# Ordering the second attention of a gated cross-attention block by whole heads

## The chip, the cores and the metric

The kernel runs on one core of a Trainium2 chip. The metric is the device time of one execution in microseconds (us). The engines are named as the profile names them: PE (TensorE, matmuls; PEld is its weight load), DVE (VectorE), ACT (ScalarE), POOL (GpSimd) and SP (SyncE, which issues all DMAs here).

## The reference

Two blocks follow one another on x of 4 x 256 tokens x 256: each is a gated cross-attention and a gated feed-forward. The change lies in the cross-attention of the second block alone:

```python
B, T_text, T_vis = 4, 256, 1601          # N_HEADS 16, N_KV_HEADS 8, HEAD_DIM 128, D_TEXT 256, D_VISION 128
x = layernorm(x) before this call
q = (text_hidden @ Wq).reshape(B, T_text, N_HEADS, HEAD_DIM).transpose(0, 2, 1, 3)
k = (vision_tokens @ Wk).reshape(B, T_vis, N_KV_HEADS, HEAD_DIM).transpose(0, 2, 1, 3)
v = (vision_tokens @ Wv).reshape(B, T_vis, N_KV_HEADS, HEAD_DIM).transpose(0, 2, 1, 3)
k, v = repeat each twice along the heads
scores = einsum('bhtd,bhsd->bhts', q, k) / sqrt(HEAD_DIM)
scores = where(mask, scores, -inf)
out = einsum('bhts,bhsd->bhtd', softmax(scores), v)
return out.reshape(B, T_text, N_HEADS * HEAD_DIM) @ Wo     # x + tanh(g) * this
```

After it comes the second feed-forward, whose three weights are quantised to three values by their mean magnitude: `silu(x @ wu.T) * (x @ wg.T) @ wd.T`.

## The kernel before, in words

Four stages follow one another: the first attention, the first feed-forward, the second attention, and the second feed-forward, with loads and preparations laid between. The second attention runs from about 725 to 1604 us of the profiled execution. In it and in the stages around it, `keep_order` ties every engine's instructions to the order in which the program writes them, so the order of the Python calls is the order on each engine.

Before this stage the weights are folded head by head: `aq` is Wq times Wk transposed and divided by sqrt(128), `vo` is Wv times Wo. So a head needs a query of 128 context channels and attends to the 128 channels of the context itself. The unit of work is a head of one batch: `units` has 4 x 16 = 64 of them, numbered u.

The work of a head, by function and line (of the kernel before):

- `project(u)`, L1335: two matmuls on PE (each runs as two passes of 32-bit data) into `ps_m`; ACT copies the query to `qT` (L1336).
- `scores(u, t)`, L1346, for eight tiles t of 32 queries: the 1601 context rows are split in four sets of 401, and the four sets fill the four quarters of the 128 partitions. Four matmuls of 32 columns lie beside each other in PE's array and write one of four `ps_sc` buffers. DVE takes the tile out (L1353): it adds the mask, negates, writes `pr` and keeps the minimum in `nm`.
- `exponentials(u, t)`, L1361: ACT makes the exponentials in place and sums them into `nm`.
- `weigh_sets(u)`: the four sets of a query have each their own maximum and sum, which have to be brought to one. It has three steps. First, SP sends `nm` by four DMAs (L1370) to `bq`, so that a query's four sets lie side by side. Second, DVE finds the common extreme (`low`, L1373) and the differences (`ws`, L1375), and ACT makes their exponential (L1376). Third, DVE makes the weighted sum, its reciprocal and the factors (L1379 to L1382), and SP sends the factors `rs` back to 128 partitions by four DMAs (L1385). In the kernel before a fourth step follows: POOL multiplies `pr` by the factors, in two halves of four tiles (L1390).
- `turn(u, half)`, L1397: DVE transposes 32 x 32 blocks of half of `pr` into `pT`. There are three `pr` and two `pT`.
- `attend(u, k)`, L1404: 13 matmuls (26 passes) of the transposed context `cx` and `pT` into one half of the bank `ps_o`. `take(u)`, L1414: ACT copies the result to `ao`.
- `project_out(u)`, L1422: two matmuls with `vo` into `ps_y`, which gathers all heads of a batch; `add_out(b)`, L1433, adds it to x.

The order around these is written by hand. Time is cut in beats of half a head (four score tiles). In each beat PE gets four tiles, and then come the steps that `place` has put into the beat, in four places: MADE, THEN, TURNED and AFTER. With k = 2u the first beat of head u, DMAs of the sums come in beat k+1, the second step in k+2, the third and POOL's multiplication in k+3, the turns in k+4 and k+5, seven and six blocks of the output in k+6 and k+7, `take` in k+7, and `project_out` in k+8.

Work of other parts is spread over the beats in the same way: `layernorm_steps` and `token_parts` of a finished batch, `prepare_mask` (L1045 to L1059) and `prepare_ctx` (L1032 to L1039: POOL copies, PE transposes, ACT copies) for the next batch, and `quantise`, 26 steps that fetch the feed-forward's weights (`w_q`, L1279), sum their magnitudes on DVE (L1286), make the scales (L1289 to L1296) and the three-valued weights on DVE (L1304, L1305). In the kernel before a step of `quantise` stands at the end of every third half beat from beat 6 on.

Of the kernel before, what the change touches and what calls it, by code (L numbers as in the profile page):

```python
# [22 lines left out]
B, S, D = 4, 256, 256  # L23
# [9 lines left out]
H = 16  # L33
# [26 lines left out]
def tile_gated_cross_blocks(ctx: ExitStack, tc: tile.TileContext, a: dict, out: bass.AP):  # L60
# [202 lines left out]
    with ExitStack() as ph:  # L263
# [413 lines left out]
        made = {}  # L677
# [568 lines left out]
    with ExitStack() as ph:  # L1246
# [80 lines left out]
        queries, found, outs, ys = ({} for _ in range(4))  # L1327
# [37 lines left out]
        def weigh_sets(u):  # L1365
# [18 lines left out]
            for i in range(SETS):  # L1384
                nc.sync.dma_start(out=factors[i * TQ : (i + 1) * TQ], in_=w[:, i])  # L1385
            yield
            for half in range(2):
# [3 lines left out]
            yield  # L1391
# [44 lines left out]

        plan = {}
# [7 lines left out]
        MADE, THEN, TURNED, AFTER = range(4)  # L1445
        for u in range(2):
            project(u)
        for u, (b, h) in enumerate(units):
            k = 2 * u
            sets = weigh_sets(u)  # L1450
            place((k + 1, AFTER), once(sets))
            place((k + 2, AFTER), once(sets))
            place((k + 3, MADE), once(sets), once(sets))
            for half in range(2):
                place((k + 4 + half, TURNED), lambda u=u, half=half: turn(u, half))
            cut = (NB1 + 1) // 2
            for half, blocks in enumerate((range(cut), range(cut, NB1))):
                place((k + 6 + half, THEN), *(lambda u=u, n=n: attend(u, n) for n in blocks))
            place((k + 7, AFTER), lambda u=u: take(u))
            place((k + 8, AFTER), lambda u=u: project_out(u))  # L1460
            if u + 2 < len(units):
                place((k + 1, AFTER), lambda u=u: project(u + 2))
            if h == H - 1:
                place((k + 9, THEN), lambda b=b: add_out(b))
                norm = layernorm_steps(b, ps_m, "ps_m")
                for i in (0, 1, 2, 3):
                    place((k + 10 + i, AFTER), once(norm))
                parts = token_parts(b)
                for i in range(4):
                    place((k + 14 + i, AFTER), once(parts))  # L1470
            if h == H - 3 and b + 1 < B:
                ready = prepare_mask(b + 1)
                place((k, AFTER), once(ready))
                place((k + 2, AFTER), once(ready))
        for b in range(1, B):
            cx = prepare_ctx(b, ps_m, "ps_m")
            for i in range(8):
                place((2 * H * b - 4 + i, AFTER), once(cx))
# [131 lines left out]
```

## Time and profile before

| what | value |
|---|---|
| runs | 1671.71 us median of 3 (1671.45 to 1672.75) |
| the profiled execution | 1674.27 us |
| its span, first to last instruction | 1672.5 us |
| mean granted clock of PE | 0.979 |
| instructions | 34286 |
| DVE, POOL busy share of the span | 71%, 39% |
| second attention: first and last start of a score matmul (L1346) | 725.2 and 1571.4 us |
| end of L1382 of the fourth and of the last head | 778.53 and 1585.69 us |

The profiled execution has its own time, some 2.6 us above the median of the runs; durations are taken from it and differences are set against the median. A row of the timeline gives the start and the length in us, the engine (SPq is SP issuing DMAs), the line, the operation, the tiles as out<-in, the shape, how many instructions are merged, and in brackets how long the engine was idle before and what ended it. A row of the chain of waits gives start, length, engine, tile and line of the work that the end was waiting for. L numbers are lines of the kernel before.

### The profile page before, as it was taken

To read this page: it belongs to the slowest core of one execution; us is meant where nothing else is said; L and a number is where in the kernel's file an instruction comes from. 1 tells how busy PE (TensorE), PEld (TensorE's weight loads), DVE (VectorE), ACT (ScalarE), POOL (GpSimd) and SP (SyncE) were. 2 spreads that over 40 slices of the span, in tenths; PEclk is the share of its full clock that TensorE was granted. 3 is DMA by queue.
4 is the path that set the end of the run, shared out by engine and by line. 5 is a ranking of instruction groups with operands and counts; after the bars stand their busy time and mean duration, and the time that the engine had idled before them with its cause. 6 is when DMAs were issued, how large, how long until landed. Compare 5 with 4: busy or idle time off the path is not lost.

```text
span 1672.5 us, 34286 instructions
## 1 busy us (share of the span) xinstructions
PE 1561.6 (93%) x13273; PEld 910.2 (54%) x13282; DVE 1191.1 (71%) x2651; ACT 782.4 (47%) x1808; POOL 660.6 (39%) x755
## 2 busy tenths in 40 slices
PE   4389799999999999989999999999999999999998
PEld 1144454454455554445666666566665666666565
DVE  6687667766867636667777787777787777777645
ACT  1235545554565553444444444445444444444334
POOL 2524514612621215524444444445444454444420
PEclk9699999999999999999999999999999999999999
DMA  4422522430424132000000000000000000000000
GB/s 109 79 44 44 77 47 44 77 56 16 77 52 94 36 96 101 1 2 15 15 15 21 21 15 8 15 21 15 15 14 2 9 2 2 2 2 2 2 1 26
DMA packets 148467, 54.07 MB, mean 32 GB/s; under 512 B 133200, under 2 KB 143952, under 8 KB 148176
## 3 DMA queue, kind: packets, MB, share of 16 engines
q1 hardware_dynamic: 148304, 51.88, 14.9%
q8 instruction: 104, 1.70, 0.4%
q14 instruction: 59, 0.48, 0.1%
HBM read 24.30 MB, written 1.05 MB: 15 GB/s over the span
## 4 chain that ended last, share of the span: by engine, by line
PE 76%; DVE 12%; POOL 3%; ACT 3%; issue 3%; DMA 2%; SPq 1%; DVEq 0%; POOLq 0%; ACTq 0%
PE ps_o L1404 22%; PE ps_sc L1346 21%; PE ps_s L689 6%; PE ps_s L650 6%; PE ps_o L711 5%; PE ps_m L1335 3%; PE ps_y L1422 3%; DVE mxs L657 3%; PE ps_m L478 2%; PE ps_v L1169 2%; PE ps_a L1183 1%; POOL pr L1390 1%; PE ps_x L1114 1%; DVE hidden L1531 1%; DVE hidden L1528 1%
## 5 line engine op out<-in xcount | busy, mean ns | idle before, releaser
L1390 POOL TENSOR_TENSOR pr<-pr,rs 128x1604 f32<-128x1604 f32 x128 | 364.0, 2866 | 473.8 <-DMA rs<-ws 417.6
L1404 PE MATMUL ps_o<-pT,cx 128*128 128x256 f32 x1664 | 394.6, 388 | 4.3 <-DVE pT L1397 4.3
L1361 ACT ACTIVATE pr<-pr,nm 128x401 f32<-128x401 f32 x512 | 319.8, 626 | 131.3 <-DVE nm L1353 107.2
L1346 PE MATMUL ps_sc<-ctxT,qT 128*32 128x401 f32 x4096 | 374.6, 506 | 4.3 <-DVE nm L1353 4.3
L1404 PEld LDWEIGHTS ps_o<-pT,cx 128*128 128x128 f32 x1664 | 307.1, 190 | 123.0 <-issue 47.2
L1353 DVE CUSTOM_DVE_ANT_0 pr<-ps_sc,mk 128x401 f32<-128x401 f32 x512 | 286.6, 573 | 96.6 <-PE ps_sc L1346 71.7
L1397 DVE STREAM_TRANSPOSE pT<-pr 128x1664 f32<-128x1664 f32 x128 | 243.5, 1902 | 103.4 <-POOL pr L1390 103.4
L657 DVE TENSOR_REDUCE mxs<-ps_s 128x2 f32<-128x768 f32 (+1 forms) x256 | 246.2, 980 | 83.3 <-PE ps_s L650 82.6
L697 ACT ACTIVATE e<-ps_s 128x1024 f32<-128x1024 f32 (+1 forms) x224 | 214.7, 964 | 174.2 <-PE ps_s L689 173.3
L1346 PEld LDWEIGHTS ps_sc<-ctxT,qT 128*32 128x32 f32 x4096 | 120.8, 110 | 205.0 <-issue 145.8
L650 PE MATMUL ps_s<-kT,qTs 64*128 64x384 bf16 (+1 forms) x1536 | 176.3, 343 | 37.4 <-DMA qTs<-qp 14.9
L689 PE MATMUL ps_s<-qTs,kT 64*128 64x256 bf16 x2496 | 174.7, 271 | 10.6 <-DVE mxs L657 10.6
L689 PEld LDWEIGHTS <-kT 64*128 64x128 bf16 x2496 | 125.3, 95 | 56.5 <-issue 22.5
L650 PEld LDWEIGHTS <-qTs 64*128 64x128 bf16 x1536 | 66.3, 97 | 136.2 <-issue 92.9
L1376 ACT ACTIVATE ws<-ws 32x32 f32<-32x32 f32 x64 | 14.6, 228 | 211.9 <-DVE ws L1375 211.9
L711 PE MATMUL ps_o<-e,vp 128*32 128x256 f32 x1664 | 112.3, 388 | 0.0
L1361 ACT ACTIVATION_READ_ACCUMULATOR pr<-pr,nm 128x1 f32 x512 | 95.4, 186 | 0.0
L711 PEld LDWEIGHTS ps_o<-e,vp 128*32 128x32 f32 x1664 | 44.5, 110 | 42.8 <-issue 25.2
L1335 PE MATMUL ps_m<-xnT,aq 128*128 128x256 f32 x256 | 65.8, 380 | 0.0
L1422 PE MATMUL ps_y<-vo,ao 128*128 128x256 f32 x256 | 65.8, 379 | 0.0
L1414 ACT COPY ao<-ps_o 128x256 f32<-128x256 f32 x64 | 23.6, 369 | 78.4 <-PE ps_o L1404 78.1
L478 PE MATMUL ps_m<-wkv,ctxg 128*128 128x512 f32 (+1 forms) x78 | 46.6, 681 | 14.0 <-ACT vp L481 8.0
(287 smaller groups left out, 1593.2 us busy)
## 6 DMA issues: line engine op xcount, KB each, us to landing
bq<-nm SPq DMA_DIRECT2D x256, 2.0 KB, 1.7
rs<-ws SPq DMA_DIRECT2D x256, 1.0 KB, 1.7
ctxT<-in_ctxT_dram SPq DMA_DIRECT2D x4, 800.5 KB, 8.0
ctxg<-in_ctxT_dram SPq DMA_DIRECT2D x16, 192.0 KB, 3.1
kT<-in_L_xattn_Wq_dram SPq DMA_DIRECT2D x4, 512.0 KB, 3.7
wo<-in_L_xattn_Wo_dram SPq DMA_DIRECT2D x4, 512.0 KB, 4.6
w_q<-in_W_upT_dram SPq DMA_DIRECT2D x8, 256.0 KB, 2.8
w_q<-in_W_gateT_dram SPq DMA_DIRECT2D x8, 256.0 KB, 2.8
```

What stands on the lines that cost most here:

```text
L650: nc.tensor.matmul(ps[:, k, :w], lhsT=qT[rows, j, i, r, :], rhs=kT[rows, 2 * s + r, c0 : c0 + w], start=j == 0, stop=j == NP - 1,)
L657: nc.vector.tensor_reduce(greatest_of[u][:, i, 2 * r : 2 * r + 2, n], ps[:, :, :w], AX.X, ALU.max)
L689: nc.tensor.matmul(ps[:, k, jj * S : (jj + 1) * S].rearrange("p (i q) -> p i q", i=QT), lhsT=kT[rows, 2 * s + r // 2, (j + jj) * P : (j + ...
L697: nc.scalar.activation(e[:, :, : nj * S], ps[:, :, : nj * S], AF.Exp)
L711: nc.tensor.matmul(summed[u][(r + k) * W : (r + k + 1) * W, :S], lhsT=vps[b % 2][:, j + jj, h * VW : h * VW + W], rhs=made[u, j, r][:, k, ...
L1335: nc.tensor.matmul(pm[:, :S], lhsT=aq[:, c, h, :], rhs=xnT[b][:, c, :], start=c == 0, stop=c == DC - 1)
L1346: nc.tensor.matmul(ps[i * TQ : (i + 1) * TQ, :KS], lhsT=queries[u][:, t * TQ : (t + 1) * TQ], rhs=ctxT[b][:, i * KS : (i + 1) * KS], start ...
L1353: nc.vector.tensor_tensor_reduce(out=prs[u % 3][:, t, :KS], in0=ps[:, :KS], in1=masks[b], scale=-1.0, scalar=3.0e38, op0=ALU.add, op1=ALU. ...
L1361: nc.scalar.activation(p, p, AF.Exp, bias=found[u][:, 0, t : t + 1], scale=-1.0, accum_out=found[u][:, 1, t : t + 1])
L1390: nc.gpsimd.tensor_tensor(p, p, bc_last(factors[:, ts], KS), ALU.mult)
L1397: nc.vector.transpose(pTs[u % 2][:, ts].rearrange("p t k -> p (t k)"), prs[u % 3][:, ts].rearrange("p t k -> p (t k)"))
L1404: nc.tensor.matmul(po[:, u % 2], lhsT=contexts[b][:, k, :], rhs=pTs[u % 2].rearrange("p t (k q) -> p t k q", q=TQ)[:, :, k, :], start=k == ...
```

## The change

The beat becomes a whole head. In beat v the order of the calls is, for v above 2: POOL's multiplication of head v-1; the eight score tiles of head v with their exponentials; the DMAs of the sums of v; `project_out` of v-3; all 13 blocks of the output of v-2; both turns of v-1; the second step of the sums of v; the steps placed BETWEEN; the third step of the sums; `take` of v-2; the query of v+2; the steps placed AFTER. The multiplication is a function of its own, `multiply`. The first heads are laid in another way: the sums of head 0 and 1 are interleaved with the tiles of the next head, and beat 2 holds the turns of head 0, the sums of head 2, the output of head 0 and the turns of head 1, in this order. `quantise` has one step in every second beat from beat 4 on, BETWEEN the second and third step of the sums; the other placed work is moved to the corresponding whole beats. No computation is added or removed.

```diff
-        queries, found, outs, ys = ({} for _ in range(4))
+        queries, found, factor_of, outs, ys = ({} for _ in range(5))
...
-            yield
+            factor_of[u] = factors
+            yield
+
+        def multiply(u):
+            factors = factor_of.pop(u)
             for half in range(2):
                 ts = slice(half * HALF, (half + 1) * HALF)
                 p = prs[u % 3][:, ts, :KS]
                 nc.gpsimd.tensor_tensor(p, p, bc_last(factors[:, ts], KS), ALU.mult)
-            yield
...
+        BETWEEN, AFTER = range(2)
+        for b in range(B):
+            last = (b + 1) * H - 1
+            place((last + 3, BETWEEN), lambda b=b: add_out(b))
+            norm = layernorm_steps(b, ps_m, "ps_m")
+            for at in ((last + 3, AFTER), (last + 4, BETWEEN), (last + 4, AFTER), (last + 5, AFTER)):
+                place(at, once(norm))
+            parts = token_parts(b)
+            for at in ((last + 6, BETWEEN), (last + 6, AFTER), (last + 7, BETWEEN), (last + 7, AFTER)):
+                place(at, once(parts))
+            if b + 1 < B:
+                ready = prepare_mask(b + 1)
+                place((last - 3, AFTER), once(ready))
+                place((last - 1, AFTER), once(ready))
+                cx = prepare_ctx(b + 1, ps_m, "ps_m")
+                for i in range(8):
+                    place((last - 3 + i // 2, (BETWEEN, AFTER)[i % 2]), once(cx))
+        background = quantise()
+        for i in range(26):
+            place((4 + 2 * i, BETWEEN), once(background))
         for u in range(2):
             project(u)
...
+        EARLY = 2
+        made, shares = range(len(units)), {}
+        for v in range(len(units) + 8):
+            if v - 1 in made and v > EARLY:
+                multiply(v - 1)
+            if v in made:
+                for t in range(TT):
+                    scores(v, t)
+                    exponentials(v, t)
+                    if 0 < v <= EARLY and t in (TT // 2 - 1, TT - 1):
+                        next(shares[v - 1])
+                shares[v] = weigh_sets(v)
+                next(shares[v])
+            if 0 < v <= EARLY:
+                multiply(v - 1)
+            if v - 3 in made:
+                project_out(v - 3)
+            if v - 2 in made and v > EARLY:
+                for k in range(NB1):
+                    attend(v - 2, k)
+            for u in [v - 1] if v > EARLY else [0] if v == EARLY else []:
+                if u in made:
+                    for half in range(2):
+                        turn(u, half)
+            if v in made and v >= EARLY:
+                next(shares[v])
+            for step in plan.pop((v, BETWEEN), []):
+                step()
+            if v in made and v >= EARLY:
+                next(shares[v])
+            if v == EARLY:
+                for k in range(NB1):
+                    attend(0, k)
+                for half in range(2):
+                    turn(1, half)
+            if v - 2 in made:
+                take(v - 2)
+            if v + 2 in made:
+                project(v + 2)
+            for step in plan.pop((v, AFTER), []):
+                step()
```

The removed half-beat plan and its loop stand in the kernel above.

More of the change, by code (lines that the diff above doesn't have):

```diff
@@ L1443, in once @@
             return lambda: next(it, None)
-        MADE, THEN, TURNED, AFTER = range(4)
+        BETWEEN, AFTER = range(2)
[15 more added lines that the diff above has]
+                    place((last - 3 + i // 2, (BETWEEN, AFTER)[i % 2]), once(cx))
@@ L1446, in tile_gated_cross_blocks @@
+        background = quantise()
+        for i in range(26):
+            place((4 + 2 * i, BETWEEN), once(background))
         for u in range(2):
             project(u)
[L1448 to L1478, printed above, removed]
-        background = quantise()
-        for i in range(26):
-            place((6 + 3 * i, AFTER), once(background))
-        beat = 0
-        while plan or beat < 2 * len(units):
-            if beat < 2 * len(units):
-                u, half = divmod(beat, 2)
-                for t in range(half * HALF, (half + 1) * HALF):
-                    scores(u, t)
-                    exponentials(u, t)
-            for where in range(4):
-                for step in plan.pop((beat, where), []):
-                    step()
-            beat += 1
+        EARLY = 2
```

## The prediction

> **What bounds the kernel now.** I read the page first (who is busy), then the stages by window, then the chain of waits, then the timeline of one head of the second attention, which is the only stage that the diff touches.
>
> ```profile
> PE 1561.6 (93%) x13273; PEld 910.2 (54%) x13282; DVE 1191.1 (71%) x2651; ACT 782.4 (47%) x1808; POOL 660.6 (39%) x755
> ```
>
> Only PE is near full over the span. By stage it is fuller still:
>
> ```profile
> 1100.00:1200.00 100.00, 100.00 (x731) 62.08 (x727) 78.68 (x195) 47.72 (x148) 46.85 (x32) 1.00 0.07 18
> ```
>
> Columns: stretch, sum, then busy PE, PEld, DVE, ACT, POOL, granted clock, DMA. In this stage PE never rests and its clock is full; DVE has a fifth free. The chain of waits says the same, one head after another:
>
> ```profile
> 1104.20 2.83 PE ps_sc L1346 x32
> 1107.03 3.22 PE ps_o L1404 x14
> 1110.25 0.86 PE ps_y L1422 x4
> 1111.12 2.83 PE ps_sc L1346 x32
> 1113.95 2.79 PE ps_o L1404 x12
> 1116.73 0.86 PE ps_m L1335 x4
> 1117.60 2.83 PE ps_sc L1346 x32
> ```
>
> A head is two rounds of four score tiles and half an output: 1117.60 - 1104.20 = 13.40 us. A second loop runs beside PE, through the sums of a head:
>
> ```profile
> 1007.66 0.18 DVE L1382 TENSOR_TENSOR ws<-ws,low 32x32 f32<-32x32 f32 x1
> ...
> 1007.91 2.41 SPq L1385 DMA_DIRECT2D rs<-ws  x4
> ...
> 1011.59 5.69 POOL L1390 TENSOR_TENSOR pr<-pr,rs 128x1604 f32<-128x1604 f32 x2 [7.94 <-DMA rs<-ws]
> ...
> 1014.49 1.91 DVE L1397 STREAM_TRANSPOSE pT<-pr 128x1664 f32<-128x1664 f32 x1 [0.71 <-POOL pr L1390]
> ...
> 1016.33 0.15 DVE L1373 TENSOR_REDUCE low<-bq 32x8 f32<-32x32 f32 x1
> 1016.51 0.80 DVE L1375 TENSOR_TENSOR ws<-low,bq 32x32 f32<-32x32 f32 x1
> ```
>
> Factors ready (L1382 ends), four DMAs, POOL multiplies both halves of pr, DVE turns the first half as soon as POOL has it, then begins the sums of the next head. DVE sits waiting for POOL there. How short this loop can be shows where PE was not the bound, for instance
>
> ```profile
> 1131.88 0.18 DVE L1382 TENSOR_TENSOR ws<-ws,low 32x32 f32<-32x32 f32 x1
> ...
> 1144.16 0.18 DVE L1382 TENSOR_TENSOR ws<-ws,low 32x32 f32<-32x32 f32 x1
> ```
>
> 12.28 us, and three times 12.27 to 12.28 at the start of the stage. So before, PE (13.39) is 1.1 us per head longer than the loop (12.28), and that 1.1 us swallows the loop's accidents.
>
> **The change part by part.**
>
> *PE, what it gains.* The instructions are the same; a head now has one round of eight score tiles instead of two of four. From the start times: score groups (four matmuls of 32 columns beside each other) follow every 0.337 us, full-width matmuls every 0.216. Entering and leaving a round costs more: 0.309 for 0.216 on entering, 0.361 for 0.337 on the first group, 0.450 for 0.337 and 0.320 for 0.216 on leaving. Sum 0.093 + 0.024 + 0.113 + 0.104 = 0.334 us a round. PE per head: 13.39 - 0.33 = 13.06; over the 60 heads of the steady stretch -20 us. That is the most the change can bring there.
>
> *The loop, what it loses.* DVE's order is now: eight L1353, both turns of the last head, low, ws, [a background step], part, low, 1/low, ws. Both turns stand ahead of the sums, so the loop now holds POOL's second half; against that, the four L1353 that stood between L1375 and L1379 (4 x 0.495) leave it, and the exponential L1376 on ACT, which they covered, enters. Behind these waits DVE has the eight L1353 of the next head queued, and behind those PE's score tiles, for want of ps_sc buffers. The new loop:
> - L1382 end to POOL start: 3.78 (median of the 64 heads)
> - both halves on POOL 5.69, to DVE 0.03
> - second turn to L1373: 1.83 (1014.49 to 1016.33)
> - L1373 to L1375: 0.23, L1375 to ACT: 0.21 or 0.83 (below), ACT and back: 0.26, L1379 to the end of L1382: 0.84.
>
> The last stretch stands alone once, in the last head:
>
> ```profile
> 1584.59 0.23 ACT L1376 ACTIVATE ws<-ws 32x32 f32<-32x32 f32 x1 [9.10 <-DVE ws L1375]
> ...
> 1584.85 0.18 DVE L1379 TENSOR_TENSOR part<-ws,bq 32x32 f32<-32x32 f32 x1 [0.29 <-ACT ws L1376]
> ```
>
> L1375 is the disputed term. It is 0.80 in 60 of 64 heads, and in the first head
>
> ```profile
> 738.77 0.18 DVE L1375 TENSOR_TENSOR ws<-low,bq 32x32 f32<-32x32 f32 x1
> ...
> 738.99 0.23 ACT L1376 ACTIVATE ws<-ws 32x32 f32<-32x32 f32 x1 [0.33 <-DVE ws L1375]
> ```
>
> 0.18. In that head POOL was idle; in the 60 it was multiplying. [...] By the common row (0.80) the loop is 3.78 + 5.69 + 0.03 + 1.83 + 0.23 + 0.83 + 0.26 + 0.84 = 13.49 and the change loses 0.1 per head at once; by the rule and the lone row it is 12.87, since L1375 now comes after a turn that has waited for POOL's end. I take 12.87.
>
> *Accidents.* The mean from L1382 to POOL is 4.00, not 3.78: in 13 of 64 heads the landing is late, as here
>
> ```profile
> 1050.55 2.41 SPq L1385 DMA_DIRECT2D rs<-ws  x4
> ...
> 1056.20 2.86 POOL L1390 TENSOR_TENSOR pr<-pr,rs 128x1604 f32<-128x1604 f32 x1 [9.02 <-DMA rs<-ws]
> ```
>
> (5.65 instead of 3.7). In nearly all of those the packet records show one 16 KB packet of the instruction queue inside the landing window; these come about every 256 instructions of PE, some 17 us apart. Before, some 52 PE instructions fall into the critical part of that window; after, PE is in the dense score round then, some 66: mean delay 0.22 x 66/52 = 0.28. Before, the 1.1 us of slack covered most of it; now the cover is gone. Loop with accidents: 12.87 + 0.28 = 13.15, against PE's 13.06. So the loop, not PE, sets the pace, narrowly. Four ps_sc buffers let PE run some 2.5 us ahead, so PE itself stalls only by the difference.
>
> *Background steps between L1375 and L1379.* They lengthen the loop by what ACT's 0.29 does not cover: 12 of L1286 at 0.65, +0.36 each, 4.3; 12 pairs L1304, L1305 at 0.45 + 0.75, +0.91 each, 10.9; the scale step +1.0; add_out (2 x 0.47) +0.65 and the xn step +0.45 in three batches, 3.3. Sum 19.5. Before, they stood where PE's excess hid them.
> *Batch changes.* The mask (1.58 on POOL, 2.0 on DVE) and the 16 copies L1032 make POOL busy under L1375 again and DVE late: by that row, 0.6 in some four heads and a remainder of the 2.0, three times; between 1 and 8, I take 4.
> *SP.* bq, then the w_q fetch (0.58 to issue), then rs, in each head: the fetch goes out while SP would wait for L1382 (479 us of such waiting in all), so 0; if its 256 KB still flows when rs starts, up to 1 us in half of the heads, which the range holds. *ACT:* take and the query copy now stand behind L1376; they end some 0.5 us before the next head's first exponential, so 0. project_out ahead of the output has a whole beat: 0. Query copies have two beats: 0.
>
> *Sum of the steady stretch.* From the end of L1382 of the fourth head to that of the last: before 1585.69 - 778.53 = 807.2. After 60 x 13.15 + 19.5 + 4 = 812.5. **+5.3.**
>
> *Start.* The first output now stands after the third head's eight tiles and needs both turns of head 0: POOL is through at 751.2, DVE turns behind the second head's sums until 755.4, and PE idles from 747.6. Following the fourth head's sums through, they end at 774.6 instead of 778.5. But the row
>
> ```profile
> 751.00:757.80 6.80, 5.93 (x33) 2.02 (x34) 6.47 (x21) 4.41 (x15) 0.21 (x2) 0.50 0.02 1
> ```
>
> shows half clock after a shorter rest (4.3 us). [...] the output of head 0 runs some 5.7 us at half clock, 2.9 lost. By row times alone -3.9, with the rule -1.0; I take **-1.0**.
> *End.* After the last L1382: 3.78 + 5.69 + 1.9 + 13 outputs of 0.43 and 0.2 = 17.2, for 18.3 before: **-1.1.**
>
> Total +5.3 - 1.0 - 1.1 = +3.2. The profiled execution took 1674.3 (span 1672.5), 2.6 above the median of the runs, 1671.7; the difference is applied to the median: **1675**.
>
> **The rivals.**
> *PE keeps the pace (faster).* If the loop with accidents stays under 13.06, every round saved counts: 60 x 13.06 + 3.8 (what PE's own extra work adds before: 807.2 - 60 x 13.39) = 787.4, -19.8, with start and end -22: 1650. The point of decision is the loop's mean at 13.06, only 0.1 below my 13.15; for it: the run-ahead of 2.5 us, and background steps in half of the heads only. Against: after a delay the loop gains back just 0.19 per head. Halfway cases end near 1662. 0.26.
> *POOL still lies over the sums (much slower).* L1375 at 0.83 and the landings at 4.0 to 4.3: loop 13.8, 60 x 13.8 + 23.5 = 851, +42: 1714. For it: 60 of 64 heads; against: the order on DVE. With half of it, 1692. 0.12.
> *No change of order.* The engine order listed for the changed kernel shows 32 score matmuls in a row and both turns together; left at 0.
>
> **How the numbers follow.** My case 0.62: 1675, with +-8 for the accidents' places and +-4 for the batch changes, 1665 to 1686. What a measurement of this kernel can tell from no change is about 0.2%, 3.3 us. My case sits on that edge: of its 0.62, slower 0.33, same 0.22, faster 0.07. With the rivals: faster 0.07 + 0.22 = 0.29 (0.04 of the first rival's 0.26 end within 0.2%, halfway and below), slower 0.33 + 0.12 = 0.45, same 0.26. The range 1660 to 1691 leaves out the far ends of both rivals.
>
> **What would show it.** L1375 at 0.18 in nearly all heads (0.80: second rival). L1382 to L1382 12.9 to 13.3 in heads without a background step, 13.7 to 13.9 with L1304. PE busy at or a little under 100% with waits at L1346 for DVE's nm; if there are none and the pitch is 13.06, the first rival is right. Half clock once more near 755, with an output of head 0 of over 8 us. I am wrong in kind if PE waits at the output for pT, or if DVE waits for bq rather than for POOL.

## The result, and the profile after

The changed kernel takes 1684.78 us (median of four runs, 1681.76 to 1687.44) where the kernel before, run beside it, takes 1672.23 (1671.45 to 1673.62): a ratio of 1.0074, 95% interval 1.0053 to 1.0094. It is slower by three quarters of a per cent; the forecast was 1675. The profiled execution is the fastest of the four, with a span of 1680.0 against 1672.5 before: 7.5 us more. From here on, L numbers are lines of the kernel whose rows are shown. In the changed kernel POOL's multiplication is L1394, the turns L1400, the output L1407, `take` L1417, `project_out` L1425 and the matmuls of the last feed-forward L1538.

The page of the changed kernel, its first row and the engines' shares of the chain that ended last:

```profile
PE 1548.1 (92%) x13274; PEld 923.0 (55%) x13282; DVE 1164.0 (69%) x2651; ACT 769.2 (46%) x1808; POOL 657.7 (39%) x755
...
PE 51%; DVE 15%; POOL 11%; issue 7%; ACT 7%; DMA 5%; SPq 3%; DVEq 0%; POOLq 0%; ACTq 0%
```

PE's busy time is 13.5 us less than before and the span is longer, so PE has begun to wait. The stretches by window, with the columns of the row shown before (stretch, sum, busy PE, PEld, DVE, ACT, POOL, granted clock, DMA):

```profile
1100.00:1200.00 100.00, 97.45 (x745) 61.96 (x738) 75.72 (x202) 47.83 (x150) 47.69 (x34) 1.00 0.06 13
1400.00:1500.00 100.00, 94.29 (x717) 59.06 (x709) 73.23 (x194) 44.15 (x144) 43.01 (x17) 1.00 0.04 7
```

The same hundred us that PE filled before now hold 2.5 of waiting, and a later hundred 5.7. The chain of waits no longer runs from one PE row to the next. In this stretch of two heads (start, length, engine, tile, line) PE does not occur:

```profile
1332.28 0.19 DVE ws L1382
...
1332.52 0.51 SPq L1385
...
1333.07 0.59 SPq L1385
...
1333.71 0.59 SPq L1385
...
1334.35 1.67 DMA rs<-ws
...
1339.00 2.88 POOL pr L1394
...
1343.73 0.16 DVE low L1373
1343.91 0.19 DVE ws L1375
1344.13 0.24 ACT ws L1376
1344.39 0.19 DVE part L1379
...
1345.06 0.18 DVE ws L1382
```

That is the loop of the forecast, 12.78 us from L1382 to L1382. In 52 of the 60 heads from the fifth on, L1373 starts right behind the second turn, as here, so nothing outside the loop held it up. What its members waited for, in the groups between 800 and 1550 us (the last column is the idle time just before them and what ended it):

```profile
L1346 PE MATMUL ps_sc<-ctxT,qT 128*32 128x401 f32 x3524 | 312.8, 504 | 15.1 <-DVE nm L1353 15.1
...
L1400 DVE STREAM_TRANSPOSE pT<-pr 128x1664 f32<-128x1664 f32 x111 | 212.1, 1911 | 139.3 <-POOL pr L1394 139.2
...
L1373 DVE TENSOR_REDUCE low<-bq 32x8 f32<-32x32 f32 x55 | 8.7, 158 | 1.8 <-DMA bq<-nm 1.7
```

DVE waits for POOL (139 us) and hardly ever for bq (1.8), and PE waits for DVE's evacuation, as the forecast had it. At the end stands a row that it did not have:

```profile
1601.50 8.86 PE L1407 MATMUL ps_o<-pT,cx 128*128 128x256 f32 x26 [3.40 <-DVE pT L1400]
```

The last output takes 8.86 us after a rest of 3.40, where the same 26 instructions take 5.78 in the heads before it. The windows of lower clock (the granted clock is the third column from the end):

```profile
751.00:757.80 6.80, 2.59 (x6) 2.14 (x7) 4.11 (x6) 0.14 (x2) 2.46 (x1) 0.50 0.03 2
1034.13:1037.54 3.41, 3.41 (x21) 0.97 (x14) 1.97 (x9) 3.21 (x11) 1.40 (x1) 0.50 0.02 1
1600.74:1607.57 6.83, 6.07 (x14) 4.88 (x15) 0.71 (x1) 0.00 (x0) 0.00 (x0) 0.50 0.00 0
```

The first was forecast (it lasts longer than before, from 750.82 to 761.06); the second comes in the midst of the stage; the third is the last output.

Where the 7.5 us of the profiled executions lie: L1382 of the fourth head ends at 777.02 (778.53 before, -1.5); from there to L1382 of the last head it is 813.05 (807.16, +5.9); from there to the end of the span 89.9 (86.8, +3.1).

### The profile page after: what moved, and what is told of

The parts are those of the page before. It is cut to its first block, busy times and chain, and to the rows that moved or that the text cites. A ratio compares the mean times of both kernels' runs of the same rounds, so it can differ in the third digit from the quotient of the medians.

```text
span 1680.0 us, 34196 instructions
## 1 busy us (share of the span) xinstructions
PE 1548.1 (92%) x13274; PEld 923.0 (55%) x13282; DVE 1164.0 (69%) x2651; ACT 769.2 (46%) x1808; POOL 657.7 (39%) x755
## 4 chain that ended last, share of the span: by engine, by line
PE 51%; DVE 15%; POOL 11%; issue 7%; ACT 7%; DMA 5%; SPq 3%; DVEq 0%; POOLq 0%; ACTq 0%
PE ps_o L1407 10%; PE ps_sc L1346 9%; POOL pr L1394 9%; PE ps_s L689 6%; PE ps_s L650 6%; PE ps_o L711 5%; ACT pr L1361 4%; DVE mxs L657 3%; DMA rs<-ws 2%; PE ps_m L478 2%; PE ps_v L1169 2%; PE ps_m L1335 2%; PE ps_y L1425 2%; SPq L1385 2%; SPq L1370 1%
## 5 line engine op out<-in xcount | busy, mean ns | idle before, releaser
L1394 POOL TENSOR_TENSOR pr<-pr,rs 128x1604 f32<-128x1604 f32 x128 | 363.8, 2864 | 445.2 <-DMA rs<-ws 282.5
L1407 PE MATMUL ps_o<-pT,cx 128*128 128x256 f32 x1664 | 375.7, 383 | 12.4 <-DVE pT L1400 12.4
L1346 PE MATMUL ps_sc<-ctxT,qT 128*32 128x401 f32 x4096 | 363.9, 504 | 15.1 <-DVE nm L1353 15.1
L1400 DVE STREAM_TRANSPOSE pT<-pr 128x1664 f32<-128x1664 f32 x128 | 244.2, 1909 | 156.6 <-POOL pr L1394 156.5
L1407 PEld LDWEIGHTS ps_o<-pT,cx 128*128 128x128 f32 x1664 | 320.2, 193 | 58.2 <-DVE pT L1400 13.7
L1353 DVE CUSTOM_DVE_ANT_0 pr<-ps_sc,mk 128x401 f32<-128x401 f32 x512 | 281.7, 571 | 56.4 <-PE ps_sc L1346 32.4
L1346 PEld LDWEIGHTS ps_sc<-ctxT,qT 128*32 128x32 f32 x4096 | 124.8, 110 | 224.1 <-issue 119.4
L1376 ACT ACTIVATE ws<-ws 32x32 f32<-32x32 f32 x64 | 14.6, 228 | 353.1 <-DVE ws L1375 353.1
L1425 PE MATMUL ps_y<-vo,ao 128*128 128x256 f32 x256 | 72.5, 406 | 1.3 <-ACT ao L1417 1.3
L1425 PEld LDWEIGHTS ps_y<-vo,ao 128*128 128x128 f32 x256 | 43.5, 189 | 46.4 <-ACT pr L1361 40.5
```

The source lines that it names most:

```text
L1346: nc.tensor.matmul(ps[i * TQ : (i + 1) * TQ, :KS], lhsT=queries[u][:, t * TQ : (t + 1) * TQ], rhs=ctxT[b][:, i * KS : (i + 1) * KS], start ...
L1353: nc.vector.tensor_tensor_reduce(out=prs[u % 3][:, t, :KS], in0=ps[:, :KS], in1=masks[b], scale=-1.0, scalar=3.0e38, op0=ALU.add, op1=ALU. ...
L1394: nc.gpsimd.tensor_tensor(p, p, bc_last(factors[:, ts], KS), ALU.mult)
L1400: nc.vector.transpose(pTs[u % 2][:, ts].rearrange("p t k -> p (t k)"), prs[u % 3][:, ts].rearrange("p t k -> p (t k)"))
L1407: nc.tensor.matmul(po[:, u % 2], lhsT=contexts[b][:, k, :], rhs=pTs[u % 2].rearrange("p t (k q) -> p t k q", q=TQ)[:, :, k, :], start=k == ...
L1425: nc.tensor.matmul(ys[b][:, i], lhsT=outs[u][:, i * P : (i + 1) * P], rhs=vo[:, h, :], start=(h, i) == (0, 0), stop=(h, i) == (H - 1, QT - 1),
```

## The experiments

Below, "rounds" are the distances between the starts of PE's outputs, head by head; 56 of them lie between the fourth output and the 60th, free of start and end. Their sum is 755.8 before and 759.1 in the changed kernel. All edits are on the changed kernel, but for one. In the edits shown, `...` stands for lines left out.

**The changed kernel again.** No edit, for its spread.

> The changed kernel itself again, for the spread of its times beside the others of this call: 1681 to 1688, as in its first four runs.

Measured: 1683.52 (1680.60 to 1689.51, six runs), ratio 1.0069 (1.0055 to 1.0083). Runs of this kernel differ by 9 us; in its profile the stretch from the fourth L1382 to the last is 816.4, with more late landings. One or two us between variants of it can't be told from medians.

**A dose in the loop.**

```diff
...
+        for v in range(4, len(units)):
+            for _ in range(2):
+                place((v, BETWEEN), lambda: nc.vector.tensor_reduce(idle_out, idle_in, AX.X, ALU.add))
```

> Two added reductions of 128x512 on VectorE (0.65 each by the row of L1286; their result is not used) between L1375 and L1379 in each of the 60 heads from the fifth on. Theory A (loop sets the pace in nearly all heads): 34 heads without background step gain 1.30 less the cover of ScalarE's exponential, 0.3 to 0.47, and 26 with one gain the whole 1.30: 34 x 0.9 + 26 x 1.3 = 64, time about 1745 to 1755. Theory B (TensorE sets the pace and the loop has about 0.5 of slack): 60 x 0.5 less, so under 35.

Measured: 1752.37 (1749.16 to 1755.36), ratio 1.0480 (1.0464 to 1.0496), so 67.6 us above the changed kernel. A head of its timeline:

```profile
918.12 0.18 DVE L1375 TENSOR_TENSOR ws<-low,bq 32x32 f32<-32x32 f32 x1
918.23 1.39 DVE L1471 TENSOR_REDUCE idle_out<-idle_in 128x1 f32<-128x512 f32 x2
919.53 0.17 DVE L1379 TENSOR_TENSOR part<-ws,bq 32x32 f32<-32x32 f32 x1
```

From L1375 to L1379 the 60 heads spend 67.7 us more than in the changed kernel, and the time grows by 67.6. That the two agree so closely is in part chance: the stretch grows by 72.5, since late landings cost 5.6 more, and start and end together are 5 shorter. But of 67.7 us put into the loop none is hidden: it sets the pace in nearly every head. This is what the forecast rests on, and the rival "PE keeps the pace" falls.

**The background steps out of the loop.**

```diff
-            place((4 + 2 * i, BETWEEN), once(background))
+            place((4 + 2 * i, AFTER), once(background))
```

> Only the place of the quantisation's 26 background steps changes: they stand behind L1382 and the output copy of a head instead of between L1375 and L1379. Theory A (the loop L1382 -> DMA -> POOL -> second turn -> sums -> L1382 sets the pace of the changed kernel): in the heads with L1286 the pitch goes from 13.05 to 12.85, in those with L1304 and L1305 from 13.7 to 12.85, so the stretch from the fourth to the last L1382 becomes 12 to 16 us shorter and the time falls from 1685 to about 1670. Theory B (TensorE, or the late landings alone, set the pace): the stretch stays within 3 us. Theory C (SP's queue matters: the w_q fetch stands ahead of the rs DMAs in the changed kernel, behind them here): the mean from L1382 to POOL falls from 4.06 as well, by 0.2 or more, and the gain exceeds 16.

Measured: 1676.24 (1673.06 to 1681.91), ratio 1.0026 (1.0018 to 1.0034): 7 to 8.5 below the changed kernel, half of what was expected. Of 16.8 us between L1375 and L1379 above the clean heads' 0.47, 14.2 are gone, but the stretch shrinks by 5.4 alone. The expectation forgot what stands close behind the loop: 5.0 us came back as waits ahead of the second turn and of L1373, most of them in eight heads where `bq` landed after the turn had ended. PE's round of 13.06, on whose scores `bq` hangs, and late landings of `bq` itself both have a part in that. Another 3.5 us came back as later landings of the factors; two profiles of the same kernel differ by 2.3 there, so whether the edit caused them is open. The mean from L1382 to POOL did not fall (4.11), so SP's queue was not the matter.

**The second turn behind the sums.**

```diff
-                    for half in range(2):
-                        turn(u, half)
+                    turn(u, 0)
...
             if v in made and v >= EARLY:
                 next(shares[v])
+            for u in [v - 1] if v > EARLY else [0] if v == EARLY else []:
+                if u in made:
+                    turn(u, 1)
```

> Only the second turn of a head is moved on VectorE, from ahead of L1373 to behind L1382; so the sums wait for POOL's first half alone. Theory A (the loop sets the pace): without POOL's second half (2.85) and with L1375 beside POOL again (0.8 instead of 0.18) the loop is about 10.6 to 11.4 and TensorE's round, predicted at 13.06, takes over: stretch 60 x 13.06 + 4 to 8 = 788 to 792 instead of 813, time about 1660 to 1663. Theory B (something else holds the heads at 13.5, so TensorE's own round or the evacuations): within 3 us of the changed kernel. Theory C (the second turn behind L1382 delays the evacuations of the next head by its 1.85 and TensorE waits for nm): gain under 10.

Measured: 1680.25 (1679.89 to 1681.47), ratio 1.0050 (1.0038 to 1.0062): a miss. The edit also moved the second turn of head 0, for which PE's first output waits: it starts at 764.31 after a rest of 17.41 (755.21 after 9.04 in the changed kernel). That loses 8.3 us up to the fourth output. Behind it the 56 rounds fall to 754.1 and the end to 75.3 from the last output's start (78.5). DVE hardly waits for POOL any more (22.8 us ahead of L1400) but for bq (141.1 ahead of L1373), and the background steps still lie in that path. L1375 stayed at 0.18, not 0.8: it now comes, behind the wait for bq, after POOL is through.

**Mended: background in the wait for bq, first heads as they were.**

```diff
-            for u in [v - 1] if v > EARLY else [0] if v == EARLY else []:
-                if u in made:
-                    for half in range(2):
-                        turn(u, half)
-            if v in made and v >= EARLY:
-                next(shares[v])
+            if v == EARLY:
+                for half in range(2):
+                    turn(0, half)
+            if v > EARLY and v - 1 in made:
+                turn(v - 1, 0)
             for step in plan.pop((v, BETWEEN), []):
                 step()
             if v in made and v >= EARLY:
                 next(shares[v])
+            if v in made and v >= EARLY:
+                next(shares[v])
+            if v > EARLY and v - 1 in made:
+                turn(v - 1, 1)
```

So VectorE now does the first turn, the background step, all sums, and then the second turn.

> On VectorE the order of a head from the fourth on is: evacuations, first turn of the head before, background steps, all sums, second turn. The first three heads stand as in the changed kernel. In the kernel with only the second turn moved the trace showed TensorE's rounds at 13.06 for long rows, VectorE idle for bq ahead of L1373 (165 us), and 10 us lost before the fourth head because head 0's second turn had moved too. Theory A (the background steps fit into the idle time before bq, and TensorE sets the pace): outputs start every 13.06 except at the batch changes (13.28 to 13.50); the stretch of 56 intervals falls from 759 to 738 to 745; time 1660 to 1668, below both kernels. Theory B (bq's landing becomes the new loop: L1382, second turn, eight evacuations, bq, sums): pitch above 13.06 in most heads and the time stays above 1672.

Measured: 1661.36 (1660.64 to 1662.76), ratio 0.9939 (0.9927 to 0.9951), as expected. Its groups between 800 and 1550 us:

```profile
L1346 PE MATMUL ps_sc<-ctxT,qT 128*32 128x401 f32 x3628 | 320.1, 504 | 4.0 <-DVE nm L1353 3.8
...
L1400 DVE STREAM_TRANSPOSE pT<-pr 128x1664 f32<-128x1664 f32 x113 | 214.7, 1900 | 9.0 <-POOL pr L1394 8.8
...
L1373 DVE TENSOR_REDUCE low<-bq 32x8 f32<-32x32 f32 x57 | 11.0, 194 | 114.4 <-DMA bq<-nm 114.3
```

PE's waiting for nm is down from 15.1 to 3.8, and DVE waits for bq, which hangs on PE's own scores. The 56 rounds take 744.1, against 754.1 with the second turn alone behind the sums.

**Two queues for the factors.** The shortest way through the same loop, with the order untouched:

```diff
             for i in range(SETS):
-                nc.sync.dma_start(out=factors[i * TQ : (i + 1) * TQ], in_=w[:, i])
+                (nc.sync, nc.scalar)[i % 2].dma_start(out=factors[i * TQ : (i + 1) * TQ], in_=w[:, i])
```

> Two of the four rs DMAs of a head (L1385) are issued on ScalarE's queue instead of SP's; the order of everything else is the changed kernel's. Theory A (the loop sets the pace): SP issued them at 0.51 + 0.59 + 0.59 in the trace, so the last one leaves about 1.1 earlier, the mean from L1382 to POOL falls from 4.06 to about 3.0, the clean pitch from 12.82 to about 11.7 or to TensorE's 13.06, whichever is longer; the stretch loses 13 to 20 us, time 1665 to 1672. Theory B (ScalarE, which now waits for L1382 before it may issue, is late with the output copy L1417 and the next exponentials): TensorE waits for ao or ScalarE's work moves behind, and half of the gain or more is lost.

Measured: 1652.10 (1650.83 to 1655.30), ratio 0.9885 (0.9870 to 0.9900): the best of all, 31 to 33 us below the changed kernel's two medians, and better than the 1665 to 1672 expected. (The stretch lost 21.2, little more than the 13 to 20 expected; the end lost another 4.6, which was not counted, and the medians lie further apart than the profiles.) A head in its timeline:

```profile
1502.97 0.18 DVE L1382 TENSOR_TENSOR ws<-ws,low 32x32 f32<-32x32 f32 x1
...
1503.18 1.16 ACTq L1385 DMA_DIRECT2D rs<-ws  x2
1503.22 1.39 SPq L1385 DMA_DIRECT2D rs<-ws  x2
...
1505.91 5.69 POOL L1394 TENSOR_TENSOR pr<-pr,rs 128x1604 f32<-128x1604 f32 x2 [6.99 <-DMA rs<-ws]
```

POOL starts 2.76 after L1382 (median 2.81, 3.79 in the changed kernel). With the loop 1.0 shorter the chain of waits is back on PE, and it is PE's new round:

```profile
1497.53 5.61 PE ps_o L1407 x26
1503.14 0.86 PE ps_m L1335 x4
1504.01 5.52 PE ps_sc L1346 x64
1509.53 1.06 PE ps_y L1425 x4
1510.59 5.61 PE ps_o L1407 x26
```

13.06 from output to output, as the forecast had computed it for PE alone. The 56 rounds take 739.8, of which 731.4 are 56 x 13.06 and over half of the rest is PE's own work at the batch changes (13.17, 13.28 and 13.50 a round). Against the changed kernel's profile: rounds -19.3, the last four heads -2.9, behind the last output -3.6 (it starts after a rest of 0.32 and takes 5.88), start -0.6: some 26.5, the difference of the spans. Of theory B, ScalarE held at L1382, only one wait of 0.9 us for ao is to be seen on PE.

**The same two queues in the kernel before.** The same line, in the kernel before:

```diff
-                nc.sync.dma_start(out=factors[i * TQ : (i + 1) * TQ], in_=w[:, i])
+                (nc.sync, nc.scalar)[i % 2].dma_start(out=factors[i * TQ : (i + 1) * TQ], in_=w[:, i])
```

> The kernel before, with two of the four rs DMAs of a head issued on ScalarE's queue, as in the changed kernel with two queues (1652.1). Theory A (before, the loop was 12.28 and hidden behind TensorE's 13.39, so a shorter loop is worth nothing; the two queues help the changed kernel only because there the loop sets the pace): outputs start every 13.39 as before, time within 3 us of 1671.7. Theory B (two queues are worth 20 us or more in any order): about 1640 to 1650.

Measured: 1668.53 (1667.33 to 1671.71), ratio 0.9978 (0.9970 to 0.9985), 4 us less than before. The 56 rounds take 755.8, as before, and the chain stays on PE's two rounds:

```profile
1106.53 2.83 PE ps_sc L1346 x32
1109.36 2.79 PE ps_o L1404 x12
1112.14 0.86 PE ps_m L1335 x4
1113.01 2.83 PE ps_sc L1346 x32
1115.84 3.22 PE ps_o L1404 x14
1119.06 0.86 PE ps_y L1422 x4
1119.92 2.83 PE ps_sc L1346 x32
```

13.39 again. None of the gain lies in the 56 rounds, as the expectation had it, though the whole is a little over its 3 us. By the profiles, which lie 7.2 us apart, 4.6 are in front, where the fourth output starts at 792.29 instead of 796.89: in the first heads the loop sets the pace before too (12.27 there, 11.28 with two queues). Another 3.1 are in the last four heads, where PE waits less for the turns. So with the loop short on both sides, the whole-head order takes 1652.1 and the order before 1668.5: the change's own gain of 16 us is real, and the loop had eaten it.

**Both: the mended order and two queues.** The two edits together:

```diff
-                nc.sync.dma_start(out=factors[i * TQ : (i + 1) * TQ], in_=w[:, i])
+                (nc.sync, nc.scalar)[i % 2].dma_start(out=factors[i * TQ : (i + 1) * TQ], in_=w[:, i])
...
+                turn(v - 1, 0)
             for step in plan.pop((v, BETWEEN), []):
                 step()
...
+                turn(v - 1, 1)
```

> The order with all sums between the two turns and the background ahead of them, and two of four rs DMAs on ScalarE's queue as well. Theory A (in that order the rs transfer is off the path: POOL's half was done 3 us before its turn): within 2 us of the same order with one queue. Theory B (late landings of rs still show there): 3 us or more faster. Theory C (ScalarE blocked at L1382 delays the exponentials): slower.

Measured: 1666.67 (1663.41 to 1673.26), ratio 0.9975 (0.9964 to 0.9986): 5 slower than with one queue. PE's waiting for nm grows to 10.3 us, in three long rounds at batch changes (15.81, 20.76, 17.64). The expectation's reason, ScalarE held at L1382, is not what the rows show. L1059 is a step of `prepare_mask` with one column, here with two queues (first two rows) and in the same order with one (last two):

```profile
1135.83 5.68 POOL L1394 TENSOR_TENSOR pr<-pr,rs 128x1604 f32<-128x1604 f32 x2 [7.39 <-ACT cx L1039]
1136.53 2.18 DVE L1059 TENSOR_TENSOR gate_b<-some,gate 128x1 f32<-128x1 f32 x1
...
1137.49 0.16 DVE L1059 TENSOR_TENSOR gate_b<-some,gate 128x1 f32<-128x1 f32 x1
1137.70 5.68 POOL L1394 TENSOR_TENSOR pr<-pr,rs 128x1604 f32<-128x1604 f32 x2 [7.39 <-DMA rs<-ws]
```

With one queue L1059 is over before POOL begins. With two, POOL begins earlier, L1059 falls beside its first multiply and ends with it, at 2.18, 2.19 and 2.26 us in the three rounds against 0.16 in every other variant of the changed kernel; the evacuations behind it are late and PE waits (4.01 us in the longest round; the mean granted clock from 800 to 1550 us is 0.99). Against one queue these three rounds are 9.0 us longer, and all 56 together 9.1.

**The tail filled.**

```diff
+            if v - 2 == len(units) - 1:
+                idle = ps_sc.tile([P, 512], F32, name="ps_sc")
+                for i in range(7):
+                    nc.tensor.matmul(
+                        idle[:, :S], lhsT=vo[:, 0, :P], rhs=ctxT[B - 1][:, :S], start=True, stop=True
+                    )
```

> Seven added fp32 products of 128x256 (14 instructions, some 3.1 us, into a score buffer that nobody reads) stand on TensorE ahead of the last output L1407, where it rested 3.40 us. Theory A (that output ran at half clock for 8.86 us because of this rest): it runs in 5.8 to 6.2 here, the granted clock stays full after 1600, and the time falls by 2.5 to 3, to about 1682. Theory B (the clock falls for another reason, or the copy and the last normalisation hide it): the output stays at 8.8 or the time does not move.

Measured: 1687.76 (1680.43 to 1691.81), ratio 1.0096 (1.0077 to 1.0114), within the changed kernel's spread, so the time settles nothing. Its timeline answers the question:

```profile
1597.84 3.18 PE L1492 MATMUL ps_sc<-ctxT,vo 128*128 128x256 f32 x14
1601.62 5.88 PE L1407 MATMUL ps_o<-pT,cx 128*128 128x256 f32 x26 [0.59 <-DVE pT L1400]
```

With PE kept busy, the same output takes 5.88 instead of 8.86: the rest had cost it 3.0. From L1382 of the last head to the end it is 88.5, only 1.4 less than the changed kernel's 89.9, since the idle products pushed seven of the feed-forward's matmuls behind the output (185 instructions there for 178), which PE then has to make up.

**The first heads not laid apart.** The lines that serve the first heads alone are taken out:

```diff
-        EARLY = 2
+        EARLY = -1
...
-                    if 0 < v <= EARLY and t in (TT // 2 - 1, TT - 1):
-                        next(shares[v - 1])
...
-            if 0 < v <= EARLY:
-                multiply(v - 1)
...
-            if v == EARLY:
-                for k in range(NB1):
-                    attend(0, k)
-                for half in range(2):
-                    turn(1, half)
```

> The first heads are not laid apart: every head from the first has the changed kernel's general order. Theory A (the start hangs on the loop alone, which runs at 12.9 from head 0 here instead of twice 10.18 and once 15.29): the fourth L1382 comes at 777 to 779, as with the heads apart (777.0), [...] time within 2 us of the changed kernel. Theory B (the special layout is worth something at the start): 3 us or more slower than the changed kernel, at the first output.

Measured: 1687.73 (1685.57 to 1688.96), ratio 1.0094 (1.0080 to 1.0108), 3 to 4 above the changed kernel. The start is not where it lies: the fourth output starts at 796.43 (797.37) and the fourth L1382 ends at 777.56 (777.02). Half clock at the first output, expected here too, did not come: that output, at 755.88, is followed by the next after 13.17 (16.04 in the changed kernel, where it takes 8.75 us). Score tiles ahead of it were slow instead (32 matmuls in 4.59 us for 2.90); the mean granted clock from 750 to 800 us is 0.97. The stretch from the fourth L1382 is 818.9 with 23.7 us of late landings (17.3 and 19.6 in the two profiles of the changed kernel). So the layout of the first heads is worth nothing at the start; whether it shifts the landings by more than chance stays open.

**Two queues, background behind, start filled.** Three edits: the two queues, the background AFTER, and idle products ahead of head 0's output.

```diff
-                nc.sync.dma_start(out=factors[i * TQ : (i + 1) * TQ], in_=w[:, i])
+                (nc.sync, nc.scalar)[i % 2].dma_start(out=factors[i * TQ : (i + 1) * TQ], in_=w[:, i])
...
-            place((4 + 2 * i, BETWEEN), once(background))
+            place((4 + 2 * i, AFTER), once(background))
...
             if v == EARLY:
...
+                for i in range(16):
+                    nc.tensor.matmul(
+                        idle[:, :S], lhsT=vo[:, 0, :P], rhs=ctxT[0][:, :S], start=True, stop=True
+                    )
                 for k in range(NB1):
                     attend(0, k)
```

> The changed kernel with three edits: two of four rs DMAs on ScalarE's queue, the background steps behind L1382 instead of inside the sums, and sixteen fp32 products of 128x256 that nobody reads (32 instructions, some 7.1 us) ahead of the first output, where TensorE rested 8.06 us and then ran 7.54 us for 5.78. Theory A: the first output runs in 5.8 and the second follows it after 13.06 instead of 14.82 (-1.8); the four rounds of 13.6 to 14.7 at quantisation steps and batch changes lose 1 to 2; time 1648 to 1650. Theory B (the rest at the start is taken back by the third head's evacuations, and the long rounds belong to mask and context copies): 1651 to 1653.

Measured: 1657.79 (1657.38 to 1658.30), ratio 0.9913 (0.9900 to 0.9926), 5.7 above two queues alone, outside both expectations. The start did what was hoped: the first output runs in 5.78, the second follows after 13.08, and the fourth starts at 792.51 instead of 796.77. Nearly all other rounds are at the floor as well. One is not: 21.24 us, at the step that forms the quantisation's scales, now behind L1382:

```profile
1130.26 5.71 POOL L1394 TENSOR_TENSOR pr<-pr,rs 128x1604 f32<-128x1604 f32 x2 [5.04 <-ACT cx L1039]
1130.34 2.84 DVE L1296 TENSOR_SCALAR qlo<-scales 128x3 f32<-128x3 f32 x1
...
1133.27 2.71 DVE L1533 TENSOR_TENSOR back<-back,gate 128x1 f32<-128x1 f32 x1
...
1136.54 4.91 PE L1346 MATMUL ps_sc<-ctxT,qT 128*32 128x401 f32 x28 [3.67 <-DVE nm L1353]
```

Two instructions on three and one columns stand 2.8 and 2.7 us beside POOL's two multiplies, the evacuations behind them are late, PE rests 3.67 and then runs at half clock (0.51 from 1135.0 to 1142.0): 7.7 us above the 13.50 of such a round. With that step left inside the sums an estimate by subtraction is 1657.8 - 7.7 = 1650; that was not run.

**Four tiles and four, with two queues.** Meant to price the row of eight by itself:

```diff
...
+                    if t == HALF - 1 and v > EARLY:
+                        if v - 3 in made:
+                            project_out(v - 3)
+                        for k in range((NB1 + 1) // 2):
+                            attend(v - 2, k)
...
-                for k in range(NB1):
+                for k in range((NB1 + 1) // 2 if split else 0, NB1):
                     attend(v - 2, k)
```

> The changed kernel with two queues for rs (1652.1, TensorE's round 13.06 nearly throughout), and on TensorE from the fourth head on four score tiles, seven blocks of the output, four score tiles, six blocks, instead of eight tiles and thirteen blocks. Theory A (entering and leaving a row of score tiles costs TensorE 0.334 once per row): round 13.39 instead of 13.06, 60 x 0.334 = 20 more, time about 1672. Theory B (the cost is hidden or smaller): under 10 more. Theory C (the later second half of the scores delays the sums as well): over 25 more.

Measured: 1877.33 (1862.30 to 1880.65), ratio 1.1209 (1.1180 to 1.1239), 225 us above two queues. It failed as a price. PE's waits:

```profile
PE ps_y L1425 <- ACT ao L1417: 131.7, 59, 3.7
```

L1425 moved ahead of half the scores, but the copy L1417 that it needs stands on ScalarE behind L1376 and the DMAs that wait for L1382 of the head before. A second loop arises, and the chain of waits runs through it: the second half of the scores, bq, the sums, L1382, ScalarE's DMAs, L1417 and L1425, 15.3 to 20.0 us from output to output. The mean granted clock of the profiled execution is 0.950, against 0.975 with two queues. The price of a round has to be read from the other runs instead: 13.39 with two rounds and 13.06 with one.

## Why the prediction was right, and where it was off

It called for slower as the likeliest sign, by the loop through the sums, and gave 1660 to 1691. The mechanism is the one that the runs show. The sign was in part luck: its +3.2 lay at the edge of what it held to be measurable, it gave slower no more than 0.45, and the largest term that it missed, the end, happened to push the same way. Its terms against the profile of the changed kernel:

- *PE's round, 13.39 to 13.06.* Right to the hundredth, in every round where PE sets the pace; the 0.334 for entering and leaving a row of score tiles holds.
- *The loop, 12.87 clean.* Measured 12.84, the mean of the 19 heads without any disturbance. L1375 is at 0.18 to 0.23 in all 64 heads, as the lone row had it; the rival that had it at 0.83 falls. One reading was wrong: POOL's second half did not enter the loop with the change. It stood in the loop before too, hidden in the 0.80 of L1375 (see the last section).
- *Accidents, 0.28 a head, 16.8 in all.* Measured 17.3 (17 late landings of 64); in the second profile 19.6. The packet records go with the forecast's reason. Between 800 and 1570 us 16 KB packets of the instruction queue come 17.4 us and 256 instructions of PE and PEld apart in the mean (17.3 and 256 before). All 17 late landings (over 0.2 us behind the median) have one between L1382 and POOL's start, and only 4 of the other 47 do (18 of 18 and 5 of 46 in the second profile). No edit that moves these packets was tried, so that they are the cause is not shown.
- *Background steps, 19.5.* Measured 16.8: a step adds some 0.1 less than counted (0.23 for the 0.36 of L1286, 0.81 for the 0.91 of L1304 and L1305; from the start of L1375 to that of L1379 a clean head takes 0.47). In the rows of the dose above, an instruction of DVE starts 0.07 and 0.09 us before the one ahead of it has ended, which fits.
- *Batch changes, 4.* Measured 7.5: 5.1 where L1379 or L1382 stand beside POOL's token steps, 2.4 where the sums wait longer than usual after the second turn.
- *The stretch, 812.5.* Measured 813.05, and its parts add up: 60 x 12.84 + 17.3 + 16.8 + 7.5 = 812.0. That the forecast is so near is in part chance, for its errors of -2.7 at the background steps and +3.5 at the batch changes cancel; none of them is large. The dose and the two queues show that it is this loop.
- *Start, -1.0.* Measured -1.5. The half clock at head 0's output came: after a rest of 9.04 us that output takes 8.75, the next one 5.78, so 2.97 are lost for the 2.9 of the forecast. To go by at the start there was one case, the window of 0.50 at 751.00 behind a rest of 4.3 us; the rule that the forecast reckons with, here and at L1375, was assumed by its author, not read from a trace.
- *End, -1.1. This step failed: it is +3.1.* The sum counted 13 outputs at full speed after a chain that leaves PE idle. By the row shown above PE rests 3.40 there, and the last output runs at half clock (0.50), 8.86 for 5.8. The half clock weighed at the start was not put to the end, though the profile before showed it there, at an output of the last heads (0.50 from 1587.23 to 1590.65):

```profile
1587.66 4.73 PE L1404 MATMUL ps_o<-pT,cx 128*128 128x256 f32 x14 [3.61 <-DVE pT L1397]
```

(14 matmuls that take 3.26 to 3.29 elsewhere.) The filled tail shows the 3.0 us: from L1382 to the end of the last output it is 17.3 there, as the forecast had it, and 20.3 in the changed kernel (18.2 before). The other 1.1 of the end's +3.1 lie behind that output: more of the feed-forward's matmuls are left there (178 of L1538, against 171 of L1518 before).

These give 5.9 - 1.5 + 3.1 = 7.5 for the profiled pair. That pair is on the kind side: the medians differ by 12.6, and by 10.8 in the repetition. That is the other half of the miss of 9.8: the forecast carried one profile's terms over to medians, and the changed kernel's runs spread wider (9 us in six) than those of the kernel before (6 us in 23). Late landings, 17.3 us in one of its profiles and 19.6 in the other, may be the reason; that is not shown.

The first rival (1650 if PE keeps the pace) was wrong for this kernel and right for the same order with the loop 1.0 us shorter: it said 1650, and that kernel takes 1652.1.

## What to carry to other kernels

When an order is changed to save time on the engine that sets the pace, compute the longest loop through the other engines too, with its accidents: here the 20 us on PE were there, but the loop with its accidents was longer than PE's new round, and what was put into it came out at the end one for one. The next step then is to shorten that loop: one line that issues two of four small transfers from a second queue was worth more than any reordering tried here. It must be tried in the order at hand: the same line lost 5 us in the mended order, where it moved POOL's work onto an instruction of one column. And where a sum leaves TensorE idle, look at what such rests cost elsewhere in the profile, at the end as well as at the start: in the changed kernel the outputs behind rests of 9.04 and 3.40 us took 8.75 and 8.86 us for 5.78, and with two queues the last one, behind a rest of 0.32, took 5.88.

## What the runs showed of the hardware

*A wait that looks like a duration.* The forecast took L1375's 0.80 before as what the instruction costs beside POOL. It is a wait: in all 60 heads with that length, L1375 ended 35 to 40 ns after POOL's second multiply (in the rows of the forecast, 1011.59 + 5.69 = 1017.28 and 1016.51 + 0.80 = 1017.31). In the other four heads no multiply of POOL ran beside it, and it took 0.18. So the loop before already held both of POOL's halves, 3.78 + 5.69 + 0.04 + four L1353 1.93 + 0.84 = 12.28; what the change put in is the second turn and the exponential in place of four L1353. Two other kernels show it with instructions that are nothing by themselves: L1059 above, 2.18 us for 0.16, and in the start-filled kernel 2.84 us for 128x3 (0.16 in the kernel before) and 2.71 for 128x1, ending as POOL's multiplies end. In the changed kernel the evacuations L1353 and the turns L1400 show no such length beside the same multiplies: at most 0.58 and 1.91 us, as elsewhere. What sets L1375, L1059, L1296 and L1533 apart from these was not tested in any run.

*SP issued the rs transfers of a head one behind the other.* It takes 0.51 to 0.59 us for each (the rows SPq L1385 in the chain above); with two on each of two queues POOL starts 0.98 earlier in the median, and this moved the kernel by 31 to 33 us.

*A clock window in mid-stage.* The half clock from 1034.13 to 1037.54 in the changed kernel comes behind a rest of only 1.97 us:

```profile
1032.88 4.40 PE L1346 MATMUL ps_sc<-ctxT,qT 128*32 128x401 f32 x32 [1.97 <-DVE nm L1353]
```

Such 32 matmuls take 2.90 us at full clock, so the rest cost 1.5 us more than its length. Other rests of up to 2.4 us in this stage brought no such window, and the kernel with two queues has none between 800 and 1600 us.
